# A two-layer graph kernel: other routes for the first loads, another order of the first steps, and a separate program for the last pair's output

## The chip, the cores and the metric

The kernel runs on one core of a Trainium2 chip. Its engines work side by side and meet at semaphores: TensorE (PE in the profile) multiplies matrices into PSUM, VectorE (DVE), ScalarE (ACT) and GpSimd (POOL) do the elementwise work, and SyncE (SP) issues most of the DMA transfers. ScalarE can issue transfers too. The metric is the device time of one execution in microseconds, the median of several runs.

## What is computed

128 graphs of 128 nodes with 512 features each go through two layers; each layer is a normalised residual. Cut to what matters, for one graph with features `x` and 0/1 adjacency `A`:

```python
# layer 0: graph attention, 8 heads of 64
feats = x @ W[h]                                        # per head
dense = leaky_relu(feats@a_self[:, None] + (feats@a_neigh)[None, :], 0.2)
att   = softmax(dense + NEG_BIG * (1 - A))
x     = layernorm(x + relu(concat_h(att @ feats) + b))
# layer 1: hypergraph convolution, twice
H, w  = (A != 0), A[0]
R     = diag(1 / (H @ w)) @ H @ diag(1 / H.sum(0)) @ H.T
h     = relu(R @ (x @ W1.T) + b1)                       # 512 -> 1024
h     = layer_norm(h) * gamma + beta
y     = R @ (h @ W2.T) + b2                             # 1024 -> 512
out   = layernorm(x + (y + x))
```

## The kernel before

The graphs go in 64 pairs. Every step of a pair (loads, features, scores, softmax, attention, hidden layer, output) is a small function with a place in time, `lag * T + time`; all are sorted by it and recorded in that order, so each engine has its instructions in one fixed order. For most pairs the large products are Winograd's: 7 block products (`chain`, with partial sums X, Y, W) in place of 8. Names to follow: `xb`, the loaded x in blocks, `xT`, its transpose; `pf`, features in PSUM, `ft`, in SBUF; `rows`/`rd`/`nb`, the neighbours' score rows, written to DRAM and read back to all partitions; `nm`, the negated maxima; `eT`, exponentials transposed; `pav`, attention; `pd`/`R`, the propagator; `pz`/`zT`/`zS`, R applied to x, and its sums; `ph`/`h`, hidden; `hS`, sums of h; `py`/`y2`, output before R; `pq`, output; `pv`, `gw`, `bw`, the means over W2 that fold the layer norm into the output weights.

The loads come by SyncE's queue. x is loaded in blocks and transposed on VectorE:

```python
    def load_blocks(p):
        ...
        rows = x[gs].rearrange("g (b n) (f c) -> f n (g b) c", b=NB, f=NB)
        for f in range(NB):
            nc.sync.dma_start(s["xb"][f * B:(f + 1) * B], rows[f])
    def x_transpose(p, s, g):
        ...
        nc.vector.transpose(
            s["xT"][:, g].rearrange("p k (b n) -> p k b n", b=NB),
            s["xb"][:, g * NB:(g + 1) * NB].rearrange("p b (f k) -> p k b f", k=KF),
        )
```

The feature weights w0 are loaded in four blocks and folded with the attention vectors (a product and a sum for each of `as_bc`, `an_bc`), and the first two pairs use them in plain products:

```python
    everywhere(as_bc, a_self, nc.scalar)
    everywhere(an_bc, a_neigh, nc.scalar)
    load_blocks(0)
    load(0)
    load_edges(0)
    ...
    def prepare_first(half):
        for n, (dst, raw, j) in ...:
            nc.scalar.copy(dst[:, :, :, 2:], raw)
            for c, bc in enumerate((as_bc, an_bc)):
                ...
                (nc.vector, nc.gpsimd)[c].tensor_tensor(t, raw, ..., op=ALU.mult)
                nc.vector.tensor_reduce(dst[:, :, :, c], t, AX.X, ALU.add)
```

Pair 0's exponentials are transposed by TensorE and copied out by ScalarE; later pairs' go by DRAM and VectorE:

```python
    def e_transpose_first(p, s):
        ...
                for h in range(HH):
                    nc.tensor.transpose(t[:, h * N:(h + 1) * N], s["nb"][:, g, n:n + N], ident)
                nc.scalar.copy(s["eT"][:, g, q * HH:(q + 1) * HH, :]..., t)
```

The last pair's output goes through the same chain as every pair's: sums `hS` (on VectorE for the last pair, on GpSimd for others), seven products, sums, the scale by the hidden layer's deviation, R, the residual, statistics, normalising, one store:

```python
    chain("py", 3, (24.2, 29.4, 27.7, 32.9, 31.2, 35.35, 37.1, 26.2, 29.6, 33.1), weigh, QU, 1)
    at(3, 31.3, y_sum, 0, 0, 0, "Y")
    ...
    @step(4, 17.0)
    def o_norm(p, s):
        for g in range(2):
            normalize(s, "o", s["o"][:, g, :], g)
        nc.sync.dma_start(out[2 * p:2 * p + 2].rearrange("g n f -> n g f"), s["o"])
    ...
            if p == PAIRS - 1:
                time = {
                    ("attend", 0): 24.25, ("attended", 0): 25.5, ("add_bias", 0): 25.6,
                    ("h_sums", 0): 19.1, ("h_sums", 1): 19.2,
                    ("product", 2): 25.0 if (lag, time) > (3, 20.0) else time,
                }.get((name,) + args[:1], time)
```

## Time and profile before

| | before |
|---|---|
| time, median of 3 runs | 2563.58 us (2562.92 to 2566.12) |
| span of the profiled execution | 2561.2 us |
| TensorE busy | 2513.8 us, 98% |
| VectorE, ScalarE, GpSimd busy | 2128.5, 1516.4, 1722.1 us |
| mean granted TensorE clock | 0.993 |
| moved by DMA | 345.04 MB, 135 GB/s on average |
| `pz` of pair 0 / of pair 1 starts | 60.75 / 113.78 us |
| last matmul starts | 2550.95 us |

A line of a timeline gives the start, the duration, the engine, the line of the kernel's source, the operation, the tiles written and read, their shape and the number of instructions merged; in brackets stands how long the engine was idle before it and what ended that. A single float matmul counts as two instructions there, a transpose as one. "Granted clock" is the share of TensorE's full clock that the chip allowed in that stretch.

### The profile page before, as it was taken

What the parts mean: (1) busy time and instruction counts of PE and PEld (TensorE: products, weight loads), DVE (VectorE), ACT (ScalarE), POOL (GpSimd) and SP (SyncE); (2) the same over time, 40 slices, a digit from 0 to 9 for tenths busy, and PEclk for the clock granted to TensorE, in tenths of its full rate; (3) what the DMA queues carried; (4) which work ended last, traced back from release to release, by engine and by line L of the source; (5) the groups of instructions that cost most, each with busy time, mean ns of one, the idle gap of its engine ahead of it and who ended that gap; (6) DMA issues with size and microseconds to landing.
All of it is one profiled execution on the core that took longest, in us unless ns stands there. A gap on an engine that the chain in (4) does not pass through costs nothing.

```text
span 2561.2 us, 48245 instructions
## 1 busy us (share of the span) xinstructions
PE 2513.8 (98%) x16316; PEld 2274.1 (89%) x16316; DVE 2128.5 (83%) x4644; ACT 1516.4 (59%) x4296; POOL 1722.1 (67%) x1802
## 2 busy tenths in 40 slices
PE   6899999999999999999999999999999999999997
PEld 4799999989989999999999998999999899998996
DVE  5788888888889888888888888888898888887875
ACT  3556656556556556556566566566565565565662
POOL 3676676766766766766766766767767666667653
PEclk8999999999999999999999999999999999999999
DMA  6444544454444444444444544444444444444430
GB/s 172 129 141 134 139 142 134 132 146 136 127 143 134 137 143 133 133 141 137 138 136 139 142 133 141 141 133 136 145 134 128 143 138 130 145 134 133 139 117 33
DMA packets 427958, 345.04 MB, mean 135 GB/s; under 512 B 146624, under 2 KB 377024, under 8 KB 427712
## 3 DMA queue, kind: packets, MB, share of 16 engines
q1 hardware_dynamic: 427424, 341.44, 45.4%
q8 instruction: 130, 2.13, 0.3%
q14 instruction: 116, 0.95, 0.1%
q10 hardware_dynamic: 288, 0.52, 0.1%
HBM read 240.14 MB, written 101.71 MB: 133 GB/s over the span
## 4 chain that ended last, share of the span: by engine, by line
PE 91%; DMA 3%; DVE 2%; issue 1%; POOL 1%; SPq 1%; ACT 0%; POOLq 0%; DVEq 0%
PE phX L741 18%; PE pyX L433 15%; PE phW L741 9%; PE pfX L433 9%; PE pyW L433 8%; PE pav L615 8%; PE phY L741 4%; PE pz L706 4%; PE pfW L433 4%; PE pq L865 4%; PE pyY L433 4%; PE pfY L433 2%; DMA nb<-rd 1%; PE pd L389 1%; DMA rd<-rows 1%
## 5 line engine op out<-in xcount | busy, mean ns | idle before, releaser
L741 PEld LDWEIGHTS phX<-zS,w_sb 128*128 128x128 f32 x3072 | 364.7, 193 | 39.4 <-issue 37.5
L535 POOL TENSOR_TENSOR nb<-nb,neg 128x512 f32<-128x512 f32 x256 | 321.3, 1277 | 111.7 <-DMA nb<-rd 65.4
L309 ACT COPY py<-pyX 128x257 f32<-128x257 f32 (+1 forms) x192 | 71.9, 374 | 547.9 <-PE pyX L433 544.7
L741 PE MATMUL phX<-zS,w_sb 128*128 128x128 f32 x3072 | 376.1, 276 | 8.8 <-issue 7.0
L792 POOL TENSOR_TENSOR sq<-sq 128x512 f32<-128x512 f32 (+2 forms) x384 | 343.5, 894 | 27.6 <-ACT sq L781 6.2
L542 ACT ACTIVATE nb<-nb,ft 128x128 f32<-128x128 f32 x1024 | 325.2, 390 | 27.5 <-POOL nb L535 25.5
L556 ACT ACTIVATE nb<-nb,nm 128x128 f32<-128x128 f32 x1024 | 320.2, 392 | 6.5 <-DVE nm L548 6.5
L662 POOL TENSOR_TENSOR rso<-veo,mhalf 128x2 f32<-128x2 f32 x64 | 44.9, 701 | 344.8 <-DVE veo L660 329.2
L646 DVE SCALAR_TENSOR_TENSOR y<-y,x 128x512 f32<-128x512 f32 x128 | 155.5, 1215 | 132.8 <-POOL y L639 132.8
L615 PEld LDWEIGHTS pav<-ft,eT 128*128 128x128 f32 x2048 | 253.5, 195 | 10.4 <-issue 1.9
L615 PE MATMUL pav<-ft,eT 128*128 128x65 f32 x2048 | 248.0, 275 | 2.1 <-DVE eT L577 1.6
L433 PE MATMUL pyX<-w_sb,hS 128*128 128x257 f32 (+1 forms) x1024 | 247.6, 384 | 2.2 <-DVE hS L415 1.8
L771 ACT ACTIVATE h<-h,b_sb 128x128 f32<-128x128 f32 x768 | 241.1, 391 | 11.4 <-DVE h L756 11.4
L433 PE MATMUL pyW<-w_sb,hS 128*128 128x256 f32 x1024 | 243.9, 380 | 3.7 <-DVE y L824 3.4
L433 PE MATMUL pyX<-w_sb,h 128*128 128x257 f32 (+1 forms) x1024 | 243.2, 379 | 0.0
L433 PEld LDWEIGHTS pyW<-w_sb,hS 128*128 128x128 f32 x1024 | 192.1, 189 | 36.6 <-DVE y L824 9.8
L433 PEld LDWEIGHTS pyX<-w_sb,hS 128*128 128x128 f32 x1024 | 189.9, 191 | 27.9 <-issue 2.1
L433 PEld LDWEIGHTS pyX<-w_sb,h 128*128 128x128 f32 x1024 | 189.2, 190 | 25.0
L639 POOL TENSOR_TENSOR y<-y,b_bc 128x512 f32<-128x512 f32 x128 | 162.3, 1268 | 61.5 <-DVE y L630 61.5
L548 DVE TENSOR_REDUCE nm<-nb 128x4 f32<-128x512 f32 x256 | 173.8, 679 | 8.6 <-ACT nb L542 6.0
L415 POOL TENSOR_TENSOR xS<-xT 128x256 f32<-128x256 f32 x124 | 118.0, 951 | 83.2 <-DVE xT L353 81.5
L309 ACT COPY ph<-phX 128x512 f32<-128x512 f32 x192 | 112.5, 586 | 94.4 <-PE phX L741 91.4
(136 smaller groups left out, 5828.8 us busy)
## 6 DMA issues: line engine op xcount, KB each, us to landing
nb<-rd SPq DMA_DIRECT2D x128, 512.0 KB, 6.4
ed<-nb SPq DMA_DIRECT2D x126, 512.0 KB, 3.2
eb<-ed SPq DMA_DIRECT2D x504, 128.0 KB, 2.9
xb<-in_x_dram SPq DMA_DIRECT2D x256, 128.0 KB, 3.0
x<-in_x_dram SPq DMA_DIRECT2D x64, 512.0 KB, 7.2
out_dram<-o SPq DMA_DIRECT2D x64, 512.0 KB, 2.9
a<-in_adj_dram SPq DMA_DIRECT2D x64, 128.0 KB, 6.5
w<-in_adj_dram SPq DMA_DIRECT2D x128, 64.0 KB, 4.3
```

Source lines behind the costliest of these rows:

```text
L309: nc.scalar.copy(t[:, :n], s[kind, "X"][:, :n])
L433: nc.tensor.matmul(to[:, :n], lhs[:, k, :], rhs[:, k, :n], start=bool(start) and k == 0, stop=(k == nk - 1), skip_group_check=True,)
L535: nc.gpsimd.tensor_tensor(t, t, neg[:, :, None, :].to_broadcast([P, NB, HH, B]), op=ALU.add)
L542: nc.scalar.activation(t, t, AF.Prelu, bias=s["ft"][:, g, h, 0:1], alpha=SLOPE)
L548: nc.vector.tensor_reduce(s["nm"][:, g, hs], scores(p, s, g, hs).rearrange("p b h j -> p h b j"), AX.XY, ALU.max, negate=True,)
L556: nc.scalar.activation(t, t, AF.Exp, bias=s["nm"][:, g, h:h + 1])
L615: nc.tensor.matmul(t[:, h * (U + 1):(h + 1) * (U + 1)], s["eT"][:, g, q * HH + h, :], s["ft"][:, g, q * HH + h, 2:], start=True, stop=True,)
L639: nc.gpsimd.tensor_tensor(s["y"][:, g, :], s["y"][:, g, :], b0_bc, op=ALU.add)
L646: nc.vector.scalar_tensor_tensor(y, y, 0.0, s["x"][:, g, :], op0=ALU.max, op1=ALU.add)
L741: nc.tensor.matmul(to[:, m * N:(m + 1) * N], w[:, k, m * P:(m + 1) * P], rhs[:, k, :], start=bool(start) and m == 0 and k == 0, stop=(k == ...
L771: nc.scalar.activation(dst[:, k, :], src[:, k, :], AF.Relu, bias=b1_sb[:, c:c + 1])
L792: nc.gpsimd.tensor_tensor(t[:, :n, :], t[:, :n, :], t[:, n:2 * n, :], op=ALU.add)
```

## The change

It touches the beginning and the end of the program and leaves the order of the pairs between as it is.

At the beginning the first two pairs' x is loaded as plain rows (the rows that the residual needs later anyway) and transposed by TensorE, so that the block loads and VectorE's transposes fall away for them. The weights w1 and w2 are issued from ScalarE's queue, ahead of and behind the neighbours' rows, and half of pair 0's rows and one of its two broadcasts go by that queue as well. The means over W2 (`pv`, then `gw` and `bw`) are taken ahead of pair 0's softmax and attention, pair 1's features too. One of pair 0's four leaky steps and three of the four evictions of its exponentials move from ScalarE to VectorE. Later loads are issued earlier.

At the end, the last pair's output weights are turned back into plain blocks (`b12`), and each graph's half is a plain product of 16 matmuls, with scale, R, residual, statistics and store by graph and by half of the columns, so that one graph's steps can stand beside the other's products. For the pair before it, a product is taken ahead of the last pair's attention, and squares and their sums come later.

```diff
+    def load_rows(p, s):
+        s["x"] = work.tile([P, 2, F], F32, tag="x", name=f"x_{p}", bufs=2)
+        nc.sync.dma_start(s["x"], x[2 * p:2 * p + 2].rearrange("g n f -> n g f"))
...
+    everywhere(an_bc, a_neigh, nc.scalar)
     everywhere(as_bc, a_self, nc.scalar)
-    everywhere(an_bc, a_neigh, nc.scalar)
-    load_blocks(0)
+    load_first(0)
+    load_rows(0, st[0])
+    for n in range(1, 4):
+        load_first(n)
+    load_rows(1, st[1])
     load(0)
     load_edges(0)
...
+    def x_transpose_first(p, s):
+        s["px"] = [bank(f"px_{p}_{g}") for g in range(2)]
+        for g in range(2):
+            for k in range(KF):
+                nc.tensor.transpose(
+                    s["px"][g][:, k * N:(k + 1) * N],
+                    s["x"][:, g].rearrange("p (f k) -> p k f", k=KF)[:, k], ident,
+                )
+
+    def x_transpose_out(p, s):
+        s["xT"] = work.tile([P, 2, KF, N], F32, tag="xT", name=f"xT_{p}")
+        for g in range(2):
+            nc.scalar.copy(s["xT"][:, g].rearrange("p k n -> p (k n)"), s["px"][g])
...
-                nc.sync.dma_start(rd[:, b, :], rows[b * B:(b + 1) * B])
+                (nc.sync, nc.scalar)[b % 2].dma_start(rd[:, b, :], rows[b * B:(b + 1) * B])
...
-            nc.sync.dma_start(dst, src.partition_broadcast(P))
+            queue = nc.scalar if p == 0 and g == 1 else nc.sync
+            queue.dma_start(dst, src.partition_broadcast(P))
...
     def leaky(p, s, g, q):
+        if (p, g, q) == (0, 1, 1):
+            ...
+            nc.vector.tensor_tensor(
+                t, t, s["ft"][:, g, hs, 0:1].to_broadcast([P, HH, N]), op=ALU.add
+            )
+            nc.vector.scalar_tensor_tensor(t, t, SLOPE, t, op0=ALU.mult, op1=ALU.max)
+            return
...
+        (nc.scalar.copy if g and q else nc.vector.tensor_copy)(
+            s["eT"][:, g, q * HH:(q + 1) * HH, :].rearrange("p h n -> p (h n)"), t
+        )
...
+    def last_weights(p, s):
+        b12 = work.tile([P, KH // 2, QU], F32, tag="hS", name="b12")
+        nc.gpsimd.tensor_tensor(b12, w2_sb[:, 4, :, :QU], w2_sb[:, 0, :, :QU], op=ALU.add)
+        s["w2"] = ((w2_sb[:, 0], b12), (w2_sb[:, 1], w2_sb[:, 2]))
...
+    for t, fn, *args in (
+        (8.0, last_weights),
+        (24.2, last_weigh, 0, 0), (27.8, last_weigh, 0, 1), (31.3, last_sum_squares, 0),
+        (31.4, last_h_rstd, 0), (31.5, last_weigh, 1, 0), (32.5, last_scale, 0, 0),
+        (32.6, last_scale, 0, 1), (34.9, last_sum_squares, 1), (35.0, last_h_rstd, 1),
+        (35.1, last_output, 0, 0), (35.2, last_output, 0, 1), (35.3, last_weigh, 1, 1, (0,)),
+        (35.5, last_o_sum, 0, 0), (35.6, last_scale, 1, 0), (36.0, last_o_sum, 0, 1),
+        (36.5, last_o_rstd, 0), (37.0, last_output, 1, 0), (37.1, last_weigh, 1, 1, (1,)),
+        (37.2, last_o_sum, 1, 0), (38.7, last_scale, 1, 1), (38.75, last_norm, 0),
+        (38.9, last_output, 1, 1), (39.6, last_o_sum, 1, 1), (40.0, last_o_rstd, 1),
+        (40.5, last_norm, 1),
+    ):
+        at(3, t, fn, *args, since=LAST)
...
-        (11.1, prepare_first, (0,)), (12.0, prepare_first, (1,)), (77.9, prepare_first_sums, ()),
+        (11.1, prepare_first, (0,)), (12.0, prepare_first, (1,)), (15.45, prepare_first_sums, ()),
+        (12.1, load_weights, (nc.scalar, w2_blocks, w2t, DH // 2, QU)),
+        (13.45, load_vectors, (0,)), (14.05, load_weights, (nc.scalar, w1_blocks, w1t, F // 2, HALF)),
+        (15.2, load, (1,)), (15.46, load_edges, (1,)), (16.1, load_vectors, (1,)),
-        (80.0, prepare_output_vectors, ()), (98.0, prepare_output, ()),
-        (112.1, prepare_output_sums, ()), (117.75, prepare_output_spread, ()),
+        (15.5, prepare_output_vectors, ()), (16.0, prepare_output, ()),
+        (79.0, prepare_rows, ()), (79.4, prepare_output_sums, ()),
+        (98.0, prepare_output_spread, ()), (98.1, prepare_output_bias, ()),
-        (122.0, prepare_output_blocks, (slice(2, 4),)),
+        (123.3, prepare_output_blocks, (slice(2, 4),)),
...
     first = {
+        ("edges", 0): 14.46, ("scale_edges", 0): 14.47, ("propagator", 0): 14.55,
+        ("spread_rows", 1): 15.72, ("nodes", 1): 15.8, ("write_nodes", 1): 15.85,
+        ("edges", 1): 15.9, ("scale_edges", 1): 15.95, ("neighbours", 1): 80.1,
+        ("propagator", 1): 98.2, ("spread_nodes", 1): 80.3, ("r_evict", 1): 110.9,
+        ("leaky", 0, 1, 1): 77.0,
+        ("masked", 1, 0, 0): 109.0, ("masked", 1, 1, 1): 121.5,
...
-            todo.append(({2: 81.0, 3: 131.0}.get(p, p * T), load, (p,)))
-            todo.append((p * T + 19.0, load_blocks, (p,)))
+            todo.append(({2: 16.3, 3: 131.0}.get(p, p * T), load, (p,)))
+            todo.append((16.2 if p == 2 else p * T + 19.0, load_blocks, (p,)))
...
-            if p == PAIRS - 1:
+            if p == LAST:
                 time = {
                     ("attend", 0): 24.25, ("attended", 0): 25.5, ("add_bias", 0): 25.6,
-                    ("h_sums", 0): 19.1, ("h_sums", 1): 19.2,
-                    ("product", 2): 25.0 if (lag, time) > (3, 20.0) else time,
+                    ("attend", 1): 25.95, ("attended", 1): 26.0, ("add_bias", 1): 26.1,
+                    ("residual", 1): 26.3, ("rstds", "a"): 26.4, ("first_shift",): 27.0,
                 }.get((name,) + args[:1], time)
+            if p == LAST - 1:
+                time = {
+                    ("product", 2): 24.22 if (lag, time) > (3, 20.0) else time,
+                    ("squares", 0): 26.5, ("squares", 1): 26.6, ("h_sums", 2): 22.3,
+                    ("sum_squares",): 43.0, ("h_rstd",): 43.2, ("y_scale", 1): 5.8, ("y_scale", 0): 5.9,
+                }.get((name,) + args[:1], time)
```

## The prediction

> **What bounds the kernel now.** I read the page first: its busy rows, its 40 slices, the chain that ended last. Then TensorE's timeline of the first 115 us and of the last 70, the busy time and granted clock in short stretches there, and ScalarE, VectorE, GpSimd and the DMA issues of the same stretches.
>
> The page's first part:
>
> ```profile
> PE 2513.8 (98%) x16316; PEld 2274.1 (89%) x16316; DVE 2128.5 (83%) x4644; ACT 1516.4 (59%) x4296; POOL 1722.1 (67%) x1802
> ```
>
> TensorE has 2561.2 - 2513.8 = 47.4 us of idle time in all. The view of stretches tells where:
>
> ```profile
> 0.00:20.00 20.00, 5.35 (x13) 4.22 (x14) 10.19 (x14) 3.76 (x5) 6.67 (x15) 1.00 0.67 151
> 40.00:60.00 20.00, 18.28 (x77) 12.00 (x76) 10.97 (x34) 5.82 (x19) 8.29 (x9) 0.66 0.77 242
> 80.00:100.00 20.00, 16.65 (x94) 15.54 (x94) 14.98 (x33) 10.52 (x30) 14.57 (x12) 0.83 0.36 95
> 120.00:140.00 20.00, 20.00 (x136) 17.90 (x134) 17.12 (x39) 12.64 (x37) 13.99 (x14) 1.00 0.50 160
> 2530.00:2540.00 10.00, 8.22 (x54) 7.13 (x53) 8.89 (x14) 6.66 (x19) 5.81 (x7) 1.00 0.15 55
> 2550.00:2562.00 12.00, 1.99 (x4) 0.68 (x4) 4.99 (x11) 0.00 (x0) 0.69 (x1) 0.75 0.12 44
> ```
>
> The numbers after the stretch's length are busy us of TensorE, its weight loads, VectorE, ScalarE and GpSimd; the last three are granted clock, DMA share and GB/s. From about 114 us to 2497 us TensorE is full at full clock: one pair takes 38.67 us there (the projection matmuls of one pair start at 2442.03, of the next at 2480.69). Nothing in the change takes a matmul out of that stretch, so only the two ends count. TensorE's timeline of the head marks its steps:
>
> ```profile
> 14.65 3.86 PE L470 MATMUL pf<-w_sb,xT 128*128 128x264 f32 x8 [14.65 <-DVE xT L353]
> 44.31 7.09 PE L615 MATMUL pav<-ft,eT 128*128 128x65 f32 x32 [0.54 <-ACT eT L592]
> 52.36 2.70 PE L241 MATMUL pv<-w_sb,gbs 128*2 128x256 f32 x8
> 60.75 2.05 PE L706 MATMUL pz<-R,y 128*128 128x128 f32 x16 [0.50 <-ACT y L683]
> 83.35 3.75 PE L741 MATMUL phX<-zS,w_sb 128*128 128x128 f32 x16 [7.01 <-issue]
> 111.94 2.00 PE L433 MATMUL pyW<-w_sb,hS 128*128 128x256 f32 x8 [1.61 <-DVE y L824]
> ```
>
> Pair 0's pz starts at 60.75, pair 1's at 113.78 when that last pyW is over: 53.0 us where a later pair takes 38.67. And the last 70 us:
>
> ```profile
> 2500.23 6.01 PE L615 MATMUL pav<-ft,eT 128*128 128x65 f32 x32 [1.58 <-DVE eT L577]
> 2517.79 1.95 PE L706 MATMUL pz<-R,y 128*128 128x128 f32 x16
> 2539.26 1.98 PE L433 MATMUL pyX<-w_sb,hS 128*128 128x257 f32 x8 [1.78 <-DVE hS L415]
> 2550.95 1.99 PE L865 MATMUL pq<-y,R 128*128 128x512 f32 x4 [1.84 <-DVE y L855]
> ```
>
> The last matmul is over near 2552.9, and 8.3 us of sums, statistics, normalising and store follow with nothing beside them.
>
> **What the skill says.** "TensorE: Matmul & The Clock Gate", Part 1, says that the array's clock falls to half after an idle window of about 3.4 us and comes back after about as long of work, the window running freely. The trace agrees on the half (granted clock 0.50 from 42 to 54, and again from 2502 to 2508 us) but not on how long an idle it takes: the 1.58 us before 2500.23 was enough, while the 1.61 us before 111.94 cost nothing. The same page, Part 4, says that transposes by TensorE land in PSUM, must be copied out, and don't count as work for the clock; here eight transposes (pet) took 2.33 us, 0.29 each, and the clock sank among them. "DMA: Bandwidth & Descriptors", Issuing engines are not separate DMA queues: SP's and ScalarE's queues share the same 16 engines, a second one saves issue time only. No run here shows the contrary: the weights move at 378 to 387 GB/s at DMA share 1.00 to 1.03 (42 to 46 us), so they get no faster. Queues, rings and completion order (same page): each ring is taken in order. The trace agrees: pair 1's 16 KB of rows took 3.88 us to land behind the weights, pair 0's 1.43.
>
> **The change, part by part: the head.** *x by TensorE.* Removed: VectorE's transposes of four blocks (2.06 us a pair) and eight loads of x in 512-byte pieces. Added: 8 transposes a pair, 8 x 0.29 = 2.3 us, and two copies by ScalarE, 2 x 0.62. By 6 us the queues had moved 0.8 MB, by 8 us 1.5 MB, so pair 0's rows (second in the queue, 1.25 MB into it) should land near 7.5 us instead of 13.33, and xT stand near 10.7. What then holds the features is VectorE's folding of w0: a block takes 0.69 + 2 x 0.65 = 2.0 us, a_self comes second now (8.1 us, where a_neigh came), so blocks are done near 10.2, 12.2, 14.1, 16.1. The first half of pair 0's features runs partly cold; eight matmuls took 6.6 us so before and take 3.7 warm. With pair 1's transposes (2 us) between, I put the end at 20.5 us, between 18.5 and 22; it was 24.6. Four us.
>
> *The wait for the broadcast.* rows written on two queues: issue 1.72 becomes 0.85 us. ScalarE's half lies behind 2 MB of w2, issued near 12 and, at some 300 GB/s beside the rest, through by 21: it lands about 23.5, the broadcasts about 27.5 to 28 (it took 4.1 us before, to 32.36). GpSimd's masking starts 4 to 4.5 us earlier.
>
> *TensorE's filling.* Pair 1's features (7.4 us), pair 0's propagator, and pv (7.9 us before, 7.2 warm) now fill about 23 to 37 us, so the clock should be full when attention starts. Before, pv stood between pav and pz, from 52.36 to 60.2, but only beside the residual's chain; it held nothing itself. *Softmax.* The fourth leaky goes from ScalarE (1.25 us) to VectorE, three of the four evictions (0.55 each) too. VectorE must now first do pair 1's nodes and edges (3.5 us), which need its `ab`, issued near 26 us, whose loads take 7.5 us in the median: 33 to 34. I expect the first maxima near 36, the last exponentials near 41.5 (43.15 before), attention over near 43.5 instead of 51.4 because it runs at full clock: 3.5 us instead of 7.1. From there bias, residual, statistics, power and scale take 2 x 1.27 + 1.74 + 1.6 + 1.9, mostly in series, 7 to 8 us (51.4 to 60.75 was 9.3). pz of pair 0 near 51: -9.7, of which I trust -7 to -13.
>
> *From pz to pz.* Waiting for the third copy of phX, TensorE stood 7.0 us and then ran cold (3.75 + 2.56 for 3.6 us of work: 2.7 more). The copy stood behind ScalarE's last exponentials, these behind a maximum, and this behind eight VectorE scalings (3.2 us) and a 3.48 us wait for pair 2's `ab`. In the new order the maximum precedes the scalings, pair 2's loads are far earlier, gw, bw and pd (2.4 us) precede pz. Following the new order by the old durations, the third copy ends 14.5 us after pz starts (22.5 before: 60.75 to 83.24), the fourth product waits 1.5 us, and two products and 22.9 to 24.5 us follow: 41 to 43 us instead of 53.0. -11.
>
> Head: -9.7 - 11 = -20.7. As TensorE is full afterwards, all of it should show in the end.
>
> **The tail.** *pyY ahead of pav* (1.74 us) fills the 1.58 us and lets pav, pyX run warm (6.01 to 3.5, 2.83 to 1.73); pm goes later (0.22). A wait of 0.47 us for the copy between pyX and pyX comes in, as the last pair had it. 1.58 + 2.5 + 1.1 + 0.2 - 0.5 = 4.9: pz at 2512.9, if y is ready; with the sums of squares behind the bias, by my count ScalarE gives it at 2511.5. The seven hidden products stay 16 us. *The last output*: 32 plain matmuls of 0.433 = 13.9 for 28 of Winograd's (12.2), +1.7; but no sums on VectorE before them (4.7 us, waits 1.78 + 0.47), and the first graph's statistics, output and store go under the second's products. Counted from the end of hidden: products and the interleaved outputs to +16.4, sum and statistics to +18, power 0.7, two halves normalised to +19.7, 128 KB stores some 3.1 where the 512 KB one took 3.9: +22.8, against 2561.2 - 2533.84 = 27.4. -4.6, with 0.2 of pm back: tail -9.3.
>
> Sum: 2563.6 - 20.7 - 9.3 = 2533.6. In the head each estimate follows one path and collisions only add, so I move it up 3: **2537**.
>
> **Rivals.** (a) *ScalarE's queue becomes the bound*: its instructions are in order, and eight weight issues (0.4 to 2.3 us each in the DMA issues of before) stand between its evictions; rows behind w2 may land at 27, not 23.5. For it: issues of w2 took up to 2.26 us once the rings were full. Against: here they start on emptier rings. It would halve the first gain: about 2543. (b) *VectorE holds softmax through pair 1's `ab`*: it stands ahead of the first maximum in the new order and has small loads. For it: before, the same wait cost 3.48 us. pz at 55: about 2541. (c) *The head's gain is lost at pz to pz*, if GpSimd (masking of pair 1, sums of z, sums of x, weights) sets the pace; it was busy 14.57 of 20 us in 80 to 100. Then only pz's 10 us and the tail remain: about 2546. (d) *All goes well*, no cold stretch: 2525. (e) The tail's clock drops anyway, or the y chain holds pz: +3.
>
> **Range and chances.** The tail is -7 to -10, the head -10 to -28, so 2525 to 2548 covers most; low 2524, high 2550. 2% is 51 us, more than the whole idle time of TensorE, so faster by over 2% needs cold time won too: 0.02. Slower by over 2% needs a stall in every pair, and steady orders are unchanged: 0.01. Same: 0.97.
>
> **What would show it.** Right: pf's first matmul near 10, pz of pair 0 near 51 and of pair 1 near 92, clock 1.00 from 30 us on, then 38.67 a pair; in the tail no idle before pav, clock 1.00, and about 23 us from the last hidden product to the end. Wrong: ScalarE's evictions waiting behind its DMA issues; the first maximum later than 38; pz to pz still over 48; clock 0.50 near attention; or a pair of over 39 us in mid-span.

## The result, and the profile after

| | before | after |
|---|---|---|
| time, median of 6 runs each | 2563.25 us (2560.77 to 2568.42) | 2557.66 us (2555.11 to 2559.59) |
| ratio, 95% interval | | 0.9975 (0.9962 to 0.9988) |
| span of the profiled execution | 2561.2 us | 2557.8 us |
| `pz` of pair 0 starts | 60.75 us | 61.27 us |
| `pz` of pair 1 starts | 113.78 us | 115.71 us |
| `pz` of the last pair starts | 2517.79 us | 2518.62 us |

The change makes the kernel faster by 0.25%. The prediction had 2537 us, with 2524 to 2550 as its range, so the result lies outside. Of the 30 us that its sum had, the head's 20.7 did not come at all; the tail's 9.3 came in good part.

The page's busy row of the changed kernel:

```profile
PE 2519.4 (98%) x16344; PEld 2281.6 (89%) x16344; DVE 2128.8 (83%) x4648; ACT 1514.0 (59%) x4291; POOL 1724.4 (67%) x1805
```

TensorE's idle time is 2557.8 - 2519.4 = 38.4 us, 9.0 less than before, but it is busy 5.6 us longer. The transposes of x are new work (16 of them, 3.1 us), and more of the work runs at half clock: up to 2550 us the granted clock is a half for 37.6 us of this trace, and for 30.7 in that of before. The view of stretches, with columns as before:

```profile
0.00:20.00 20.00, 11.01 (x48) 9.05 (x48) 9.54 (x18) 5.31 (x9) 7.09 (x15) 1.00 0.83 236
...
40.00:60.00 20.00, 16.11 (x56) 11.76 (x56) 14.01 (x28) 6.59 (x20) 7.41 (x9) 0.55 0.66 121
80.00:100.00 20.00, 15.46 (x63) 12.88 (x63) 13.24 (x26) 6.83 (x20) 13.13 (x12) 0.75 0.27 68
120.00:140.00 20.00, 20.00 (x142) 18.11 (x141) 17.71 (x39) 14.36 (x43) 13.35 (x15) 1.00 0.49 159
2530.00:2540.00 10.00, 9.88 (x57) 8.38 (x58) 8.31 (x15) 7.71 (x22) 4.27 (x5) 1.00 0.04 15
```

In the first 20 us TensorE works twice as much as before (11.01 us for 5.35). From 40 to 60 us it has less work left to do, and still does it at clock 0.55, where 0.66 was granted before. The head in TensorE's timeline (start, duration, engine, line, operation, tiles, shape, count, idle before and its releaser):

```profile
9.93 2.76 PE L497 MATMUL pf<-w_sb,xT 128*128 128x264 f32 x8 [0.16 <-ACT xT L386]
...
41.79 2.48 PE L625 MATMUL pet<-ident,nb 128*128 128x128 f32 x8 [3.85 <-issue]
...
46.39 3.51 PE L649 MATMUL pav<-ft,eT 128*128 128x65 f32 x16
...
61.27 3.79 PE L740 MATMUL pz<-R,y 128*128 128x128 f32 x16 [2.35 <-ACT y L717]
...
90.17 2.10 PE L460 MATMUL pfX<-w_sb,xS 128*128 128x264 f32 x4 [4.51 <-ACT pf L325]
...
113.87 2.00 PE L460 MATMUL pyW<-w_sb,hS 128*128 128x256 f32 x8 [1.28 <-DVE y L857]
115.71 1.95 PE L740 MATMUL pz<-R,y 128*128 128x128 f32 x16
```

The features start 4.7 us earlier, and by 41.79 all that is gone: TensorE has stood 3.85 us, 8 matmuls of `pav` (one graph; x16 in the line, as float matmuls count twice) take 3.51 us, and `pz` starts 0.5 us later than before. From there to pair 1's `pz` are 54.44 us (53.03 before), with a new stop of 4.51 us before a `pfX` in place of the old one of 7.01 before `phX`. The tail:

```profile
2504.44 3.68 PE L649 MATMUL pav<-ft,eT 128*128 128x65 f32 x32
...
2510.47 1.97 PE L460 MATMUL pyX<-w_sb,hS 128*128 128x256 f32 x8 [0.56 <-ACT py L325]
...
2516.81 1.97 PE L460 MATMUL pyW<-w_sb,hS 128*128 128x256 f32 x8 [0.91 <-POOL sq L826]
2518.62 1.95 PE L740 MATMUL pz<-R,y 128*128 128x128 f32 x16
...
2551.65 0.70 PE L977 MATMUL pq<-y_last,R 128*128 128x256 f32 x2 [0.57 <-DVE y_last L969]
```

`pav` takes 3.68 us (6.01 before) with no idle ahead of it. From the `pz` of the pair before the last (2484.79) to the end are 73.0 us, where the kernel before has 80.5 (2480.69 to 2561.2). Part of this is how the clock fell in that one execution of before. head_alone, a kernel of the experiments below that has the old tail and the same idle time, ran the same `pav` at full clock:

```profile
2501.51 3.76 PE L649 MATMUL pav<-ft,eT 128*128 128x65 f32 x32 [1.58 <-DVE eT L614]
```

From its `pz` of the pair before the last to its end are 79.4 us, so in the traces the new tail is worth between 6.4 and 7.5.

The profiled difference is then 1.9 us lost up to pair 1's `pz`, 2.2 lost over the pairs between, 7.5 won in the tail: 3.4 in all, as the spans say.

### The profile page after: what moved, and what is told of

It reads as the page before. It is cut to its first block, busy times and chain, and to the rows that moved or that the text cites. A ratio compares the mean times of both kernels' runs of the same rounds, so it can differ in the third digit from the quotient of the medians.

```text
span 2557.8 us, 48296 instructions
## 1 busy us (share of the span) xinstructions
PE 2519.4 (98%) x16344; PEld 2281.6 (89%) x16344; DVE 2128.8 (83%) x4648; ACT 1514.0 (59%) x4291; POOL 1724.4 (67%) x1805
## 4 chain that ended last, share of the span: by engine, by line
PE 91%; DMA 4%; DVE 2%; issue 1%; POOL 1%; ACT 1%; SPq 0%; ACTq 0%; POOLq 0%; DVEq 0%
PE phX L775 18%; PE pyX L460 14%; PE pfX L460 9%; PE phW L775 9%; PE pav L649 8%; PE pyW L460 8%; PE pz L740 5%; PE phY L775 4%; PE pfW L460 4%; PE pq L898 4%; PE pyY L460 4%; PE pfY L460 2%; DMA nb<-rd 1%; PE pd L416 1%; DMA dnb<-dd_d 1%
## 5 line engine op out<-in xcount | busy, mean ns | idle before, releaser
L325 ACT COPY py<-pyX 128x257 f32<-128x257 f32 x189 | 70.6, 374 | 539.3 <-PE pyX L460 535.7
L460 PE MATMUL pyX<-w_sb,hS 128*128 128x257 f32 x1008 | 242.7, 383 | 0.6 <-ACT py L325 0.6
L460 PE MATMUL pyX<-w_sb,h 128*128 128x257 f32 x1008 | 240.0, 380 | 0.0
L585 DVE TENSOR_REDUCE nm<-nb 128x4 f32<-128x512 f32 x256 | 173.6, 679 | 1.9 <-POOL zS L763 1.3
```

Of the source, the lines that this page charges most:

```text
L325: nc.scalar.copy(t[:, :n], s[kind, "X"][:, :n])
L460: nc.tensor.matmul(to[:, :n], lhs[:, k, :], rhs[:, k, :n], start=bool(start) and k == 0, stop=(k == nk - 1), skip_group_check=True,)
L585: nc.vector.tensor_reduce(s["nm"][:, g, hs], scores(p, s, g, hs).rearrange("p b h j -> p h b j"), AX.XY, ALU.max, negate=True,)
```

## The experiments

Times are medians beside runs of the kernel before on the same chip; the ratio is to those. "pz 0" and "pz 1" are the starts of the projection of pairs 0 and 1 in the profiled execution; their difference is what the second half of the head is measured by. The last column is what follows pz 1.

| kernel | time, us | ratio (95%) | pz 0 | pz 0 to 1 | pz 1 | pz 1 to end |
|---|---|---|---|---|---|---|
| before | 2563.25 | 1 | 60.75 | 53.03 | 113.78 | 2447.4 |
| after | 2557.66 | 0.9975 (0.9962 to 0.9988) | 61.27 | 54.44 | 115.71 | 2442.1 |
| tail_alone | 2553.14 | 0.9959 (0.9944 to 0.9974) | 60.19 | 52.65 | 112.84 | 2439.9 |
| head_alone | 2565.48 | 1.0016 (1.0009 to 1.0022) | 61.99 | 53.27 | 115.26 | 2445.9 |
| w1_by_sync | 2551.15 | 0.9949 (0.9933 to 0.9966) | 52.91 | 54.36 | 107.27 | 2441.7 |
| kept_warm | 2558.96 | 0.9982 (0.9974 to 0.9990) | 62.76 | 54.31 | 117.07 | 2439.3 |
| vector_order | 2559.86 | 0.9985 (0.9978 to 0.9992) | 63.03 | 53.07 | 116.10 | 2443.0 |
| no_scalings | 2552.07 | 0.9963 (0.9953 to 0.9974) | 54.38 | 53.33 | 107.71 | 2445.7 |
| sums_by_gpsimd | 2554.80 | 0.9974 (0.9961 to 0.9986) | 55.34 | 55.21 | 110.55 | 2445.0 |
| sync_order_gpsimd | 2552.19 | 0.9960 (0.9945 to 0.9975) | 53.75 | 53.24 | 106.99 | 2442.5 |
| y_sums_first | 2552.44 | 0.9961 (0.9947 to 0.9975) | 53.93 | 51.10 | 105.03 | 2445.7 |
| quiet_gpsimd | 2546.91, one run | | 54.01 | 50.89 | 104.90 | 2440.2 |
| relieved | 2551.42, one run | | 54.06 | 49.43 | 103.49 | 2445.9 |
| quiet_relieved | 2550.43, one run | | 58.48 | 45.51 | 103.99 | 2444.7 |
| all_sums_by_vector | 2546.34 | 0.9932 (0.9915 to 0.9949) | 53.26 | 49.22 | 102.48 | 2441.4 |

Two things on reading it. Each row shows one profiled execution, and kernels with the same head differ there: pz 0 to 1 by 0.4 us between before and tail_alone, and by 1.2 between after and head_alone. pz 0 is 61.27 to 63.03 in the four kernels that have the changed head with w1 on ScalarE's queue, and 52.91 to 55.34 in eight of the nine that have it on SyncE's (quiet_relieved is the ninth). So a step of 8 us in pz 0 is clear, and one of about a microsecond in either column is not told from scatter. The total is told less well still: what follows pz 1 has the same instructions in all thirteen kernels with the new tail, with nothing left out there, and runs from 2439.3 to 2445.9 us, because 25 to 38 of the later pairs start over 0.1 us late, by up to 2.1 (largely the same pairs in every run). Where those waits come from was not tried. A shorter stretch from pz 0 to 1 is also paid for in part by the next: from `pz` of pair 1 to that of pair 2 are 38.7 to 39.3 us in most kernels, but 39.7 to 40.2 in y_sums_first, relieved, quiet_relieved and all_sums_by_vector. And the profiles of after and before are one execution each, so that 1.9 and 2.2 us above are not to be explained further.

### Which half brings the gain

The first kernel is the old one with only the last pair's new output and the order around it; the later one is the new head with the old tail.

> The kernel before with only the end of the change: the last pair's output as plain products by graph, and the new places of the last two pairs' steps. If the end brought what the change brings and the beginning nothing (my theory), this is 6 to 9 us below the kernel before, ratio about 0.997, the same as the whole change; pav of the last pair at full clock without a wait, some 22 us from the last hidden product to the end. If instead the beginning brought the gain and the end none, the ratio is 0.9995 to 1.0005.

> The changed head with the tail of before: what tail_alone leaves out. If head and tail add up (after 2557.7, tail alone 2553.1, before 2562.9), the head alone costs 4.5 us: 2565 to 2569, ratio about 1.0017. If head and tail act on each other, or the difference between after and tail_alone is scatter, it comes to 2561-2564.

Measured: 0.9959 (0.9944 to 0.9974) with the tail alone, 1.0016 (1.0009 to 1.0022) with the head alone. The medians of before beside them are 2562.87 and 2561.84 us. So all of the gain is the tail's, 9.7 us (6.7 to 14.4 by the interval), and the head, on which two thirds of the prediction rested, makes the kernel slower, by 3.6 us (2.3 to 5.6), of which the traces show 1.5 to 1.9 up to pair 1's `pz`. The two about add up: 9.7 won and 3.6 lost would be 6.1, and 5.6 are measured.

### Pair 0: ScalarE behind its own transfers

ScalarE's timeline of the changed kernel; ACTq lines are transfers that it issues.

```profile
23.93 0.45 ACTq L127 DMA_DIRECT2D w_sb<-in_w1t_dram  x1
24.41 0.49 ACTq L127 DMA_DIRECT2D w<-in_w1t_dram  x1
30.60 3.74 ACTq L127 DMA_DIRECT2D w_sb<-in_w1t_dram  x2
34.38 0.66 ACT L507 COPY ft<-pf 128x264 f32<-128x264 f32 x2 [12.53 <-DMA w<-in_adj_dram]
34.93 1.28 ACT L579 ACTIVATE nb<-nb,ft 128x128 f32<-128x128 f32 x4
```

Two issues of w1's 512 KB blocks take 0.45 and 0.49 us. The third comes only at 30.60 and the fourth at 33.97 (the line of 3.74 us spans both), and ScalarE, whose instructions are in order, copies nothing before 34.38, although the first of those features were ready at 29.2 (VectorE copied its half of them then). What the last two issues waited for is in the trace. The fourth issue, and, from the view of DMA issues, how long two transfers took from issue to landing:

```profile
33.97 0.37 ACTq L127 DMA_DIRECT2D w_sb<-in_w1t_dram  x1
...
w_sb<-in_w1t_dram ACTq DMA_DIRECT2D x1, 512.0 KB, 6.6
...
w<-in_adj_dram SPq DMA_DIRECT2D x1, 64.0 KB, 9.0
```

The first transfer is w1's own first block, issued at 23.93 and landed at 30.58; the second is a load of the adjacency on SyncE's queue, issued at 24.97 and landed at 33.94. In the records of this trace the transfers of these microseconds signal their ends on eight semaphores, which both queues use over and over, and these two issues wait for the transfer that had their semaphore before: w1's third issue came 0.02 us after the first of these landings, its fourth 0.03 us after the second. head_alone shows the same (landed 31.74 and 34.70, issued 31.76 and 34.72). So the 12.53 us that the profile puts down to a small load of the adjacency are put down rightly: ScalarE stood at an issue that waited for another engine's transfer, and its copies stood behind. The test issues the same four transfers from SyncE, behind pair 1's small loads:

```diff
-        (14.05, load_weights, (nc.scalar, w1_blocks, w1t, F // 2, HALF)),
-        (15.2, load, (1,)), (15.46, load_edges, (1,)), ...
+        (15.2, load, (1,)), (15.46, load_edges, (1,)),
+        (15.47, load_weights, (nc.sync, w1_blocks, w1t, F // 2, HALF)), ...
```

> The changed kernel with w1 issued by SyncE after pair 1's adjacency loads instead of by ScalarE. Theory (ScalarE's instructions stood behind its own stalled w1 issues, from 24.9 to 34.4 us): the copies of pair 1's features are over by 31.5 us, pair 1's rows by 32, the first exponentials start at 36 to 37 instead of 41.3, pet then follows pv with little or no idle, the clock stays at 1.00 and pz of pair 0 starts near 51 to 53 instead of 61.3. Rival (VectorE is held by pair 1's adjacency or by GpSimd, whatever ScalarE does): the first exponentials stay at 40 or later, pz at 59 or later. What pair 1's pz gains is open: near 10 if nothing else bounds, 5 or less if VectorE's backlog does.

ScalarE's timeline of this kernel:

```profile
23.52 0.36 ACTq L544 DMA_DIRECT2D nb<-rd  x1
29.09 0.38 ACT L507 COPY ft<-pf 128x264 f32<-128x264 f32 x1 [6.45 <-DMA w<-in_adj_dram]
...
31.15 3.61 ACT L579 ACTIVATE nb<-nb,ft 128x128 f32<-128x128 f32 x12
```

The copy comes 5.3 us earlier, the first maximum at 36.85 (40.58), and pair 0's `pz` at 52.91: 8.4 us earlier than in the changed kernel, and near the 51 that the prediction had. The time falls to 0.9949 (0.9933 to 0.9966). Nothing of w1's transfer itself got faster: its first sums on GpSimd still wait for it, till 39.89. pz 0 to 1 stays at 54.36, so that stretch has another cause.

The edit moved three things at once, and not all of the 3.7 us at the first maximum is the copies' doing. VectorE's last instruction ahead of it, in the changed kernel and in w1_by_sync:

```profile
38.35 2.31 DVE L407 TENSOR_SCALAR hB<-hT,deg 128x128 f32<-128x128 f32 x2
...
36.45 0.48 DVE L407 TENSOR_SCALAR hB<-hT,deg 128x128 f32<-128x128 f32 x2
```

In the changed kernel GpSimd's first sums of w1 run from 38.04 to 40.38, beside it; in w1_by_sync they begin at 39.89, after it. 1.8 of the 3.7 us lie there. Also, pair 1's `ab`, whose loads wait in SyncE's order in the same way, landed at 36.21 in the changed kernel and at 31.52 here. VectorE used it at 36.93, so that wait, the prediction's own choice, was less than a microsecond from being the one that held, and no kernel tells what the copies alone were worth.

### Pair 0: the half clock in attention

The 8.4 us at `pz` are more than the 3.7 at the first maximum: from there to `pz` are 20.7 us in the changed kernel and 16.1 in w1_by_sync, where `pav` also runs at full clock: 1.90 us for 8 matmuls, not 3.51. I took the idle 3.85 us ahead of `pet` for the cause of the half clock and filled it with nine more matmuls, whose results nobody reads:

```diff
         t = bank(f"pet_{g}{q}")
+        if (g, q) == (0, 0):
+            for _ in range(9):
+                nc.tensor.matmul(t[:, :FW], ident, w0_sb[:, 0, 0]..., start=True, stop=True)
```

> The changed kernel with nine extra matmuls (results overwritten) in TensorE's idle 3.85 us ahead of pet. Theory (the clock at one half from 43 to 66 us comes from this idle and lengthens the way to pz): clock 1.00 there, pav 1.75 us a half instead of 3.5, pz of pair 0 at 56 to 58 instead of 61.3. Rival (the way to pz is set by GpSimd and VectorE and the cold clock costs little): pz at 60 or later. Pair 1's pz by 0 to 4 us earlier.

TensorE's timeline of this kernel:

```profile
38.95 4.27 PE L625 MATMUL pet<-w_sb,ident 128*128 128x264 f32 x18
44.26 2.33 PE L631 MATMUL pet<-ident,nb 128*128 128x128 f32 x8 [1.03 <-issue]
46.77 1.30 PE L631 MATMUL pet<-ident,nb 128*128 128x128 f32 x4 [0.18 <-issue]
47.87 3.52 PE L655 MATMUL pav<-ft,eT 128*128 128x65 f32 x16
```

The idle time is filled, and `pav` takes 3.52 us all the same: my theory fell. The view of stretches of this kernel, with columns as before:

```profile
43.74:47.15 3.41, 2.65 (x10) 1.38 (x10) 3.38 (x6) 3.33 (x11) 0.00 (x0) 1.00 0.82 127
47.15:50.56 3.41, 3.41 (x17) 3.15 (x17) 2.50 (x6) 1.57 (x6) 0.00 (x0) 0.50 0.01 2
```

The clock is 1.00 to 47.15 us and a half from there, just before `pav` (47.87). The bounds of these two stretches are not chosen freely. In each of the fifteen traces the granted clock changes only at places that are whole multiples of 3.41 us apart: in the changed kernel at 21.64, 25.06, 42.12, 66.02, 89.91 and 100.15, which are 1, 5, 7, 7 and 3 such steps. So I measured how much TensorE multiplied in the step before each fall to a half, and in the weakest steps after which it stayed full:

- The clock fell after steps without any multiplication (changed kernel 38.71 to 42.12, before 36.97 to 40.38, and the one above, which holds 2.65 us of transposes and nothing else), and after steps with 0.99 us (changed kernel, to 21.64), 1.10 (quiet_gpsimd, to 79.12), 1.36 (all_sums_by_vector, to 97.33) and 1.50 (before, to 26.73).
- It stayed full after 1.54 (head_alone, from 84.84), 1.57 (tail_alone, from 20.94) and more. The edge is not sharp: it stayed after 1.80 (before, from 108.65) and fell after 1.84 (before, from 2497.98), where head_alone has 1.86 in the same place and stayed.
- Transposes count for something, but less: with 2.0 to 2.5 us of them in the step, 0.7 to 1.4 us of multiplications were enough (relieved from 40.15, w1_by_sync from 39.52). Matmuls over two rows (`gw`, `bw`) hardly count: sync_order_gpsimd fell after a step that was full of work (45.20 to 48.61), 1.3 us of it `pav` and most of the rest these.

So by these traces the clock asks for some 1.5 to 1.8 us of multiplication in each step of 3.41, with no transposes beside it. The nine matmuls were over at 43.22, just before the step that begins at 43.74. In w1_by_sync the exponentials come close together, and no step is left without multiplications; the late copy draws them apart. That working came after the runs; no kernel was made to test it alone.

### From pz to pz: the order on VectorE

In the changed kernel the last `h` sum stands on VectorE at 87.78, though its product is over at 81.8; `skip`, pair 2's nodes and two sums of w2 are ahead of it, and TensorE's 4.51 us before `pfX` hang on it. This kernel puts it ahead:

```diff
-        ("nodes", 2): 130.0, ("write_nodes", 2): 130.1, ... ("skip", 0): 128.5,
+        ("nodes", 2): 138.15, ("write_nodes", 2): 138.2, ... ("skip", 0): 136.5,
-        (132.0, prepare_output_block_sums, (nc.vector, slice(2, 4))),
+        (132.5, prepare_output_block_sums, (nc.vector, slice(2, 4))),
```

> The changed kernel with VectorE's last sum of pair 0's hidden layer ahead of the residual skip, of the nodes of pair 2 and of two sums of the w2 blocks. Theory (that sum, ready at 81.9 us, stood behind 8 us of other VectorE work until 87.8, ScalarE's next copies behind it, and TensorE idled 4.5 us and then ran cold): the sum comes by 83, the 4.5 us wait before pfX is under 1 us, the clock stays at 1.00 from 80 to 100, pz of pair 1 starts at 106 to 109 instead of 115.7, pz of pair 0 stays near 61; total 6 to 9 us below the changed kernel. Rival (GpSimd or the transfers set the step from pz to pz): another wait of 3 us or more takes its place and pz of pair 1 stays at 113 or later.

TensorE's timeline of this kernel:

```profile
87.26 1.05 PE L460 MATMUL pfX<-w_sb,xS 128*128 128x264 f32 x4
...
112.64 3.62 PE L460 MATMUL pyW<-w_sb,hS 128*128 128x256 f32 x8 [5.94 <-DVE y L857]
116.10 1.95 PE L740 MATMUL pz<-R,y 128*128 128x128 f32 x16
```

The wait is gone and the stretch is 53.07: 1.4 us of the 4.51, hardly more than the scatter. A wait of 5.94 us further on has taken its place, again for VectorE. The rival on record, another wait in its stead, held.

### From pz to pz: VectorE's own work

If the order does not matter, the amount might. VectorE is busy 42.54 of the 54.44 us. This kernel is w1_by_sync without the 16 scalings of w2 by gamma (6.5 us); gamma is thus left out of the output.

```diff
-        (117.8, prepare_output_blocks, (slice(0, 1),)),
-        (118.1, prepare_output_blocks, (slice(1, 2),)),
-        (123.3, prepare_output_blocks, (slice(2, 4),)),
```

> The changed kernel with w1 issued by SyncE, and without the 16 scalings of w2 by VectorE (0.41 us each, 6.5 us together); w2 is used as loaded, so gamma is left out of the output. Theory (between the first two propagations it is VectorE's whole work, 42.5 us busy of 54.4, that sets the time, not its order): the stretch from pair 0's propagation to pair 1's falls from 54.4 to 48-50.5 us, and the time from 2551 to about 2546. Rival (other waits, GpSimd's masking and squares or TensorE's lower clock, keep the stretch): 52.5 us or more, and a time within 2 us of 2551.

The stretch is 53.33 us, only 1.0 less, which is within the scatter. VectorE's timeline of this kernel:

```profile
70.00 4.86 DVE L728 SCALAR_TENSOR_TENSOR o<-y,b_bc 128x512 f32<-128x512 f32 x2
74.78 1.35 DVE L341 SCALAR_TENSOR_TENSOR w<-a,w 128x128 f32<-128x128 f32 x1
...
79.88 0.68 DVE L790 TENSOR_TENSOR h<-ph,phW 128x512 f32<-128x512 f32 x1
```

and GpSimd's:

```profile
69.36 2.18 POOL L211 TENSOR_TENSOR w_sb<-w,w_sb 128x1024 f32<-128x1024 f32 x1
71.62 2.69 POOL L211 TENSOR_TENSOR w_sb<-w_sb 128x1024 f32<-128x1024 f32 x1
74.27 3.20 POOL L826 TENSOR_TENSOR sq<-sq 128x512 f32<-128x512 f32 x3
```

VectorE reached `skip` (L728) while GpSimd was at its sums of w2, and the two instructions took 4.86 us, where w1_by_sync has 2.85; L341 took 1.35, not 0.28. A third of the time taken away came back as longer instructions: VectorE's busy time fell by 4.4 us (43.09 to 38.67), not by 6.5. Most of the rest became idle time of VectorE, and the last `h` sum comes 25.5 us after `pz`, instead of 26.5.

Two further kernels moved work instead: the last two sums of w2 from VectorE to GpSimd, alone and together with the order above.

```diff
-        (132.0, prepare_output_block_sums, (nc.vector, slice(2, 4))),
+        (126.6, prepare_output_block_sums, (nc.gpsimd, slice(2, 4))),
```

> The changed kernel with w1 issued by SyncE, and the two last sums of w2 (3.1 us on VectorE, ahead of the last h sum) on GpSimd, which has an idle 1.96 us there. Theory (VectorE's whole work): the stretch from pair 0's propagation to pair 1's falls from 54.4 to 51-52.5 us, the time from 2551 to about 2548.5. Rival: GpSimd's squares and h sums, put off by 4.3 us, become the wait: 54 us or more, 2551 or more.

> The three together: w1 issued by SyncE, the last two sums of w2 on GpSimd, and the h sums ahead of skip and of pair 2's nodes on VectorE. Theory (VectorE's whole work): what the moved sums take off is kept, 50-52 us from propagation to propagation, and the time is 2546-2549, the lowest of the complete kernels. Rival (order and sums only move the waits on): 53 us or more, 2551.

Both missed: 55.21 and 53.24 us, nothing gained, or 1.1 us, which is within the scatter. 3.2 us less on VectorE were worth nothing clear when GpSimd had some 5 us more. This fits two engines that hold each other up, and does not show it.

### From pz to pz: VectorE beside a busy GpSimd

This is the decisive pair with no_scalings. VectorE gets 2.4 us more to do, GpSimd's two sums of w2, and GpSimd's sums of pair 0's squares are left out (pair 0's output is scaled wrongly, and gamma is out as before), so that GpSimd is idle while VectorE works up to the last `h` sum.

```diff
-        (126.5, prepare_output_block_sums, (nc.gpsimd, slice(0, 2))),
+        (131.9, prepare_output_block_sums, (nc.vector, slice(0, 2))),
     def squares(p, s, g, level):
+        if p == 0:
+            return
```

> As no_scalings, with GpSimd kept idle while VectorE works up to the last h sum: GpSimd's two sums of w2 are done by VectorE instead (two instructions more for it, 1.2 us each where nothing runs beside them), and the sums of pair 0's squares (5.9 us of GpSimd) are left out, so that pair 0's y is scaled wrongly. Theory (VectorE's instructions with two SBUF inputs are held up by GpSimd's, as the Trainium skill says on its page 'SBUF — State Buffer', section 'Who interferes with whom'; in no_scalings L728 took 2.1 and 2.8 us and L341 1.35): L728 takes about 0.7 us each, L341 0.28, and the last h sum starts 77.5-78.5, earlier than the 79.9 of no_scalings although VectorE has 2.4 us more to do. Rival (VectorE's own work only): durations as before, the last h sum at 82 or later.

VectorE's timeline of this kernel:

```profile
69.97 1.29 DVE L728 SCALAR_TENSOR_TENSOR o<-y,b_bc 128x512 f32<-128x512 f32 x2
71.17 0.28 DVE L341 SCALAR_TENSOR_TENSOR w<-a,w 128x128 f32<-128x128 f32 x1
...
77.08 0.68 DVE L790 TENSOR_TENSOR h<-ph,phW 128x512 f32<-128x512 f32 x1
```

It begins L728 at the same time as no_scalings, has two instructions more, and is done 2.8 us earlier. The durations alone changed: 1.29 for 4.86, 0.28 for 1.35. So the holdup is shown. It agrees with what the expectation cites from the Trainium skill, for L728 and L341 read two operands from SBUF, and GpSimd's sums read SBUF; which of the two waits for which, these durations do not show. Nor is it only instructions with two such operands: L407, above, scales one operand by a value per row, and its two runs took 2.31 us beside GpSimd's sums and 0.48 without. The reduction to the maxima (L585, one operand) takes 0.69 us in this run both beside GpSimd's sums of z (at 59.68) and with GpSimd idle (at 63.67). pz 0 to 1 is 50.89, 2.4 less than no_scalings. How much of that is VectorE's earlier end, and how much GpSimd's being free earlier for its later steps, this pair does not divide.

### Peeling, and a kernel that uses it

The last three kernels ask whether these parts add up. y_sums_first is sync_order_gpsimd with pair 3's nodes behind pair 0's `y` sums and pair 1's `rsa` ahead of a mask; relieved leaves the scalings out as well; quiet_relieved also has all w2 sums on VectorE and no sums of pair 0's squares.

```diff
-        ... ("nodes", 3): 150.0, ("write_nodes", 3): 150.1, ...
+        ... ("masked", 2, 0, 0): 147.4, ("nodes", 3): 152.2, ("write_nodes", 3): 152.3, ...
```

> sync_order_gpsimd, with the chain peeled that held it: pair 3's nodes (3.6 us on VectorE) behind pair 0's y sums instead of ahead of them, and pair 1's rsa ahead of the next pair's first mask on GpSimd. Theory (the wait of 8.3 us before pyW is this order on VectorE): pz to pz falls from 53.2 to 49-50.5 us, and the time from 2552 to 2547.5-2550. Rival (yet another chain ends within a microsecond of it): 52 us or more, the time as sync_order_gpsimd's.

> y_sums_first without the 16 scalings of w2 (gamma left out of the output): order, sums and VectorE's work together. Theory (several chains through VectorE and GpSimd end close together, so that only taking them away together helps): pz to pz 46-48.5 us, where the scalings alone gave 1.0 us and order and sums alone 1.1. Rival (a chain that none of these touches, pair 1's masks to its softmax to pav): 49.5 us or more, within 1 us of y_sums_first.

> relieved and quiet_gpsimd together: no scalings of w2, no sums of pair 0's squares (gamma and pair 0's scale are left out of the output), all four sums of w2 on VectorE, and the order of y_sums_first. Theory (the parts add up: what holds the stretch is VectorE's and GpSimd's work taken together, with the holdups between them): pz to pz 46-48 us, against 49.4 of relieved and 50.9 of quiet_gpsimd. Rival (a chain that none of them touches, pair 1's softmax to its last sums): 49 us or more.

y_sums_first came to 51.10, between what the theory and the rival had; the wait before `pyW` fell from 8.28 to 5.82 us and did not go. relieved came to 49.43, 0.9 us above the theory's range, but 1.7 below y_sums_first, where the rival had it within 1 (its other bound, 49.5 or more, is not told from 49.43). Together, quiet_relieved, the stretch is 45.51: the parts do add up, and no chain at 49 us stops it. (Its pair 0 started late, at 58.48, since its `pav` ran cold. Pair 1's chain was late by as much: its masks and sums of x stand 4.4 us later than quiet_gpsimd's, so the stretch can be compared, the total not.)

In a complete kernel nothing can be left out, but work can be put where it holds up less. all_sums_by_vector is y_sums_first with all four sums of w2 on VectorE ahead of the last `h` sum: 9.1 us less for GpSimd, 4.9 more for VectorE.

```diff
-        (126.5, prepare_output_block_sums, (nc.gpsimd, slice(0, 2))),
-        (126.6, prepare_output_block_sums, (nc.gpsimd, slice(2, 4))),
+        (131.9, prepare_output_block_sums, (nc.vector, slice(0, 2))),
+        (131.95, prepare_output_block_sums, (nc.vector, slice(2, 4))),
```

> y_sums_first with all four sums of w2 on VectorE, a complete kernel: GpSimd has 9.1 us less to do and VectorE 4.9 us more, ahead of the last h sum. Theory (instructions of the two hold each other up): pz to pz 50-51.5 us, not above the 51.1 of y_sums_first by more than 0.5, and the time 2550-2553. Rival (VectorE's own work counts alone): 53 us or more.

TensorE's timeline of this kernel:

```profile
53.26 3.52 PE L740 MATMUL pz<-R,y 128*128 128x128 f32 x16 [4.81 <-ACT y L717]
...
77.72 1.13 PE L460 MATMUL pfX<-w_sb,xS 128*128 128x264 f32 x4 [1.04 <-ACT pf L325]
...
98.91 3.78 PE L460 MATMUL pyW<-w_sb,hS 128*128 128x256 f32 x8 [3.63 <-DVE y L857]
```

The stretch is 49.22, better than either theory had it, with *more* work on the engine that is in the way: four instructions more, and VectorE is busy 42.95 us of the stretch, where y_sums_first has 42.46; GpSimd is busy 32.23 instead of 40.06. The time is 2546.34 us, 0.9932 (0.9915 to 0.9949) of the kernel before: the lowest median of a complete kernel here, clearly faster than the changed kernel (0.9962 to 0.9988) and than before, and not quite clear of w1_by_sync (0.9933 to 0.9966). A wait of 3.63 us for VectorE is left before `pyW`, and it still drops the clock.

## Why the prediction failed, and where it held

*x by TensorE* (features done at 20.5): held, and better. The features end at 19.0 us.

*The wait for the broadcast* (masking 4 to 4.5 us earlier): nearly held. It starts at 28.66 for 32.36, 3.7 us earlier.

*Softmax* ("the first maxima near 36", `pz` of pair 0 near 51, of which I trusted 7 to 13 us): failed. The maximum came at 40.58 and `pz` at 61.27. The step that failed is the wait that was taken to set it, VectorE's for pair 1's `ab`, until 33 to 34. ScalarE set it: the copies of pair 1's features stood till 34.38 behind its own issues of w1, which waited for earlier transfers to land, and VectorE's L407 then took 2.31 us for 0.48. `ab` itself landed at 36.21, later than predicted, but still 0.7 us before VectorE came to it. Rival (a) named ScalarE's eight weight issues but looked for the loss at the rows behind w2, and there it did not happen (the rows' issues stand at 19.83, w2's took 0.38 to 0.52 each); and it would have cost half the gain, where issuing w1 from ScalarE cost 8.4 of the 9.7 us predicted. "Emptier rings" asked the wrong thing: the issues were short, 0.37 to 0.49 us, and what they waited for was the landing of other transfers.

*The clock* ("should be full when attention starts"): failed through the same step, as the late exponentials left a step of 3.41 us without multiplications. With w1 by SyncE it was full, and `pz` came at 52.91. The working also doubted the free-running window because 1.58 us of idle time were enough in one place and 1.61 were not in another. By the traces the length of the idle stretch is not what counts: the steps of 3.41 us around these two hold 1.84 and 1.80 us of multiplications, both near the edge.

*From pz to pz* (41 to 43 us, minus 11): failed, and not through the same cause: it was 54.36 with pair 0 mended. What the prediction followed, the third copy of phX, came nearly as it said: it was over 15.4 us after `pz` (14.5 predicted, 22.5 before), and the fourth product waited 1.00 us, where it had 1.5, for 7.01 before:

```profile
76.77 2.02 PE L775 MATMUL phX<-zS,w_sb 128*128 128x128 f32 x16 [1.00 <-POOL xS L442]
```

The step that failed is "two products and 22.9 to 24.5 us follow", the old trace's remainder taken over as it stood. It was 34.0 us from the end of those two products (81.7) to `pz` of pair 1, 9.5 to 11 too many. 4.51 of them are the wait before `pfX`, for the `h` sum that stood on VectorE until 87.78, and some 5 (an estimate: half of the 10.24 us that the clock was a half, from 89.91) are the clock that fell in that wait. Work on VectorE that had lain in the old wait now lay after it, and its instructions got longer beside GpSimd's. Removing that one wait gave only 1.4 us (vector_order), so other chains ended close behind it. Rival (c) said so, with GpSimd as the pace; it was neither engine alone but the two together: 45.51 with the order changed and work of both taken away, 53.33 and 55.21 with one relieved by itself. Which of those chains sets the last microseconds stays open.

*The tail* (9.3): held: 9.7 us by the times (6.7 to 14.4), 6.4 to 7.5 in the traces. `pz` to `pz` gave 3.3 (37.10 to 33.83) where 4.9 was predicted; mis-sized was the last pair's chain of products, for which a wait of 0.47 was allowed and 0.56 and 0.91 came, which is 1.0 of the missing 1.6; and 1.1 of the 3.3 come from the cold `pav` of before, as head_alone's 36.00 shows. From the last hidden product to the end are 22.3 us (2535.5 to 2557.8), 22.8 predicted.

*"Collisions only add, so I move it up 3"*: that allowance should have been what one missed chain costs. Rivals (a) and (c) together, which is what happened, were never put together: they give no gain in the head, and 2563.6 - 9.3 = 2554.

The profile of before had the sign. The view of one source line, for `skip` (L694 there), gives the shortest, median and longest of its runs in ns:

```profile
L694 DVE SCALAR_TENSOR_TENSOR o<-y,b_bc x128: 676/1178/1222, 83.9 to 2524.7; 128x512 f32<-128x512 f32 x128
```

The instruction takes 0.68 us alone and 1.18 in the median. I took old durations from whichever place they stood in, as if each were the instruction's own.

## What to carry to other kernels

An issue of a transfer is an instruction of the engine that issues it, and in these traces it waits until some earlier transfer, of another queue even, has landed: before moving transfers to a computing engine's queue, ask what stands behind the last of them in that engine's order and which landing it may have to wait for, and give them to an engine that has nothing else to do. Where two engines hold each other up, relieving one of them may be worth little and moving work from one to the other nothing; compare the shortest and the median duration of an instruction to see it. And when a wait goes, what lay in its shadow has to be laid out anew before its length is counted as gain.

## What was not expected of the hardware

- Two issues on ScalarE's queue that stood 5.7 and 3.0 us, each until an earlier transfer had landed, one of them a 64 KB load that SyncE had issued (landed 30.58 and 33.94, issued 30.60 and 33.97).
- TensorE at half clock after a step of 3.41 us with transposes only, even with nine multiplications just before it (kept_warm, `pav` 3.52 us). "TensorE: Matmul & The Clock Gate" in the Trainium skill, Part 4, says that transposes don't count as work for the clock in the same way. The traces agree in that 2.65 us of transposes alone did not keep it; they also show that transposes are not nothing, as 2.5 us of them beside 0.7 to 0.8 of multiplications kept it in relieved.
- Idle stretches of TensorE do not tell by their length what the clock does: 2.43 us (changed kernel, ahead of `pf` at 21.41), 2.68 (quiet_gpsimd, `pfX` 2.10 us for 1.05) and 3.63 (all_sums_by_vector) ended at half clock, and so did 1.58 in the kernel before, while 1.58 in head_alone and 2.03 in tail_alone did not. The multiplications in the step of 3.41 us tell all of these but the ones near the edge.
- VectorE's instruction on 128x2 values, `sh` (L711), takes 1.21 us in the changed kernel, on the way to pair 0's `pz`, where it begins at 59.16 just after a mask on GpSimd (59.09), and 0.16 in quiet_relieved before pair 1's `pz`, where it begins (97.75) ahead of the mask (97.84): a holdup of a microsecond for an instruction that does almost nothing.
